# Toeplitz matrices of a token-mixing layer: 64 written rows per channel, or 16 table rows read at four offsets

## The chip, the cores and the metric

The kernel runs on one core of a Trainium2 chip. A core has TensorE (matmul), VectorE (DVE), ScalarE (ACT), GpSimd (POOL) and SyncE (SP), a fast memory SBUF of 128 partitions, accumulation banks PSUM, and 16 DMA engines that move data between DRAM and SBUF. SP computes nothing; it issues DMAs in the order of its program, and POOL issues some as well. The metric is the time of one execution in device microseconds.

## The reference

Four layers follow each other on an image batch x of shape (8, 56, 56, 192), all in float32. Before each layer x is group-normalized, and each layer's result is added to x. Layers 0 and 1 are gated Toeplitz layers and are the ones concerned here; layer 2 is a depthwise 7x7 convolution with an MLP, layer 3 is windowed attention.

A Toeplitz layer widens 192 channels to 576:

```python
p = silu(x @ p_w.T + p_b)
qv = silu(x @ q_w.T + q_b) * silu(x @ v_w.T + v_b)
a1 = _rpe_mlp(rpe_input, ...) * decay      # one value per lag and channel
a2 = _rpe_mlp(rpe_input, ...) * decay
o1 = _toeplitz(qv along w, a1)
o2 = _toeplitz(qv along h, a2)
out = (p * (o1 + o2)) @ o_w.T + o_b
```

For one channel c and one line of 56 points, `_toeplitz` gives `o[i] = sum_j a[i - j, c] * qv[j]`, with lags from -55 to 55. So each channel has its own 56x56 matrix in each of two directions, and every matrix is made from 111 values.

## The kernel before, in words

Samples are handled in pairs, four pairs in all; `j0` is 0 or 2 and names the two pairs that a stage works on. Layers are called L0 and L1 in the code.

**The stages of a Toeplitz layer.** `tno_qv` (here Q) loads x, normalizes it on ACT, multiplies by the weights `wq` on TensorE (L262, or L283 for the first tokens), adds the bias on DVE (L271, L290), takes SiLU on ACT (L300), multiplies q by v on POOL (L303) and stores the product to `qv` in DRAM through SP (L306). A store is issued just ahead of the ACT step of the unit after it. The tile for the product comes from a pool of three buffers.

`tno_toeplitz` (TZ) works through n = 0 to 17: nine blocks of 64 channels, and for each block d = 0 (along w) and d = 1 (along h). For each n it loads the products `q` (at even n with two DMAs, L378, in runs of 512 bytes; at odd n with one, L381) and the matrices `tm` (L388). For every channel TensorE takes two 56x32 pieces of its matrix as weights (L401): partition r holds row r of the Toeplitz matrix, so the piece `tm[rows, at:at + 32]` has a different shift in each partition. Two channels stand one below the other, in partitions 0 to 55 and 64 to 119. ACT copies the result (L408), DVE transposes it (L419, L421), POOL adds the second direction (L423) and stores the sum (L433). `tms` holds two tiles; the load for n + 2 is issued as n ends, after q's load for n + 2.

`tno_out` (O) loads the sums (L498) and x (L119), makes the gate p, multiplies, projects back with `ow`, adds x and stores.

**The tables.** `decay_tables` runs the small MLP for all 111 lags on TensorE and DVE, and writes `a`, a tile of 128 channels and 112 columns, from a pool of two buffers (`name="a"`, L186). There are five such tiles for each of two directions and two layers, 20 in all, the fifth of each with 64 channels. Each is stored to `tables[d]` in DRAM with one DMA (L198).

`expand_tables` then builds the matrices in DRAM with DMAs from DRAM to DRAM (L206): for 32 channels at once, 64 rows of 32 x 56 values, where row r is the table from lag entry r on. There are 18 such DMAs per table and four tables, 72 in all. Their source reads each run of 56 values (224 bytes) at its own offset.

**The order of the work.** `weave` interleaves generators by their estimated times: a lane of Q and O stages is run, and steps of TZ (or of `expand_tables`) are given out in proportion. In `tno_layers` the lanes are: Q(0,0) with the input statistics, the tables and `expand_tables`; then Q(0,2) with TZ(0,0); O(0,0) and Q(1,0) with TZ(0,2); O(0,2) and Q(1,2) with TZ(1,0); O(1,0) with TZ(1,2); and O(1,2) with the start of the convolution. In the first lane the order on each engine is set by a planner that goes by its own cost estimates. From the first TZ to the last, the four compute engines keep the order in which the code is written; SP's is still the planner's. Nothing reorders a queue at run time: an instruction that waits holds up all behind it on its engine.

Of the kernel before, what the change touches and what calls it, by code (L numbers as in the profile page):

```python
# [12 lines left out]
F32 = mybir.dt.float32  # L13
# [13 lines left out]
B, H, W, C = 8, 56, 56, 192  # L27
# [4 lines left out]
D1 = 576  # L32
# [11 lines left out]
class Net:  # L44
# [86 lines left out]

    def decay_tables(self, L, p, tables):

        nc, inp = self.nc, self.inp
        tv = p.tile([32, 111], F32, name="tv", bufs=1)
        nc.sync.dma_start(tv, inp["tvec"])
        pows = []
        for c in range(5):  # L140
            m = min(128, D1 - 128 * c)
            sl = p.tile([128, 1], F32, name="sl")
            nc.sync.dma_start(sl[:m], inp[f"{L}_slope"][128 * c : 128 * c + m, :])
            nc.vector.tensor_scalar(sl[:m], sl[:m], 0.0, 1.0, ALU.max, ALU.min)
            nc.vector.tensor_scalar(sl[:m], sl[:m], 1.0 - 0.95, 0.95, ALU.mult, ALU.add)
            pw = p.tile([128, 64], F32, name="pw", bufs=5)
            nc.gpsimd.memset(pw[:m, 0:1], 1.0)
            n = 1
            while n < 64:
                nc.vector.tensor_scalar(  # L150
                    pw[:m, n : 2 * n], pw[:m, 0:n], sl[:m], None, ALU.mult
                )
                n *= 2
                if n < 64:
                    sq = p.tile([128, 1], F32, name="sl")
                    nc.vector.tensor_mul(sq[:m], sl[:m], sl[:m])
                    sl = sq
            pows.append(pw)
        for d in range(2):
            t = f"{L}_t{d + 1}"  # L160
            w0 = p.tile([32, 2], F32, name="w0")
            nc.sync.dma_start(w0[:, 0:1], inp[f"{t}_w0"])
            nc.sync.dma_start(w0[:, 1:2], inp[f"{t}_b0"])
            ws = p.tile([32, 3, 32], F32, name="ws")
            nc.sync.dma_start(ws, inp[f"{t}_ws"])
# [5 lines left out]
            nc.sync.dma_start(bo, inp[f"{t}_bo"])  # L171
            h = p.tile([32, 111], F32, name="h")
            nc.vector.tensor_scalar(h, tv, w0[:, 0:1], w0[:, 1:2], ALU.mult, ALU.add)
            nc.vector.tensor_scalar(h, h, 0.0, None, ALU.max)
            for i in range(3):
                hp = self.bank2()[:32, 0, :111]
                nc.tensor.matmul(hp, ws[:, i, :], h, start=True, stop=True)
                h = p.tile([32, 111], F32, name="h")
                nc.vector.tensor_scalar(h, hp, bs[:, i : i + 1], 0.0, ALU.add, ALU.max)
            for c in range(5):  # L180
                m = min(128, D1 - 128 * c)
                ap = self.bank2()[:, 0, :111]
                nc.tensor.matmul(
                    ap[:m], wo[:, 128 * c : 128 * c + m], h, start=True, stop=True
                )
                a = p.tile([128, 112], F32, name="a")  # L186
                nc.gpsimd.memset(a[:m, 111:112], 0.0)
                back = view(pows[c][:m], 55, [[-1, 55]])
                for lo, hi, dec in ((0, 55, back), (55, 111, pows[c][:m, 0:56])):
                    nc.vector.scalar_tensor_tensor(  # L190
                        view(a[:m], 110 - lo, [[-1, hi - lo]]),
                        ap[:m, lo:hi],
                        bo[:m, c : c + 1],
                        dec,
                        ALU.add,
                        ALU.mult,
                    )
                nc.sync.dma_start(tables[d][128 * c : 128 * c + m, :], a[:m])  # L198

    def expand_tables(self, tables, mats):  # L200


        for tab, mat in zip(tables, mats):
            for n in range(D1 // 32):
# [159 lines left out]
    def tno_toeplitz(self, j0, mats, qv, o):  # L364
# [19 lines left out]
        def matrices(n):  # L384

            blk, d = divmod(n, 2)
            of = mats[d][2 * blk : 2 * blk + 2].rearrange("n p e -> (n p) e")
            nc.sync.dma_start(self.tms[n % 2][:, : 32 * H], of)  # L388

        def along(n, q, ot, g):  # L390


            d, tm = n % 2, self.tms[n % 2]
            pt = self.bank2()
            for hf in range(2):
                for j in range(4):
                    c = 4 * g + j
                    at = c * H + (28 if d else 24) * hf
                    for r in range(2):
                        rows = slice(64 * r, 64 * r + 56)  # L400
                        nc.tensor.matmul(  # L401
                            pt[32 * j : 32 * j + 32, r, hf * 224 : (hf + 1) * 224],
                            tm[rows, at : at + 32],
                            q[rows, :, 4 * c : 4 * c + 4],
                            start=True,
                            stop=True,
                        )
# [257 lines left out]
    def tno_layers(self, x0, x1, x2, gn, last):  # L665
# [3 lines left out]
        LS = ("L0", "L1")  # L669
        tables = [  # L670

            [self.dram.tile([D1 + 1, 112], F32, name=f"{L}_tab{d}") for d in range(2)]
            for L in LS
        ]
        mats = [
            [self.dram.tile([D1 // 32, 64, 32 * H], F32, name=f"{L}_mat{d}") for d in range(2)]
            for L in LS
        ]
        qvs = {
# [5 lines left out]
        with ExitStack() as ctx, ExitStack() as wqp:  # L685
# [4 lines left out]
            TZ = lambda i, j0: self.tno_toeplitz(j0, mats[i], qvs[j0], o[i])  # L690
            QT, OT, TZT = 25 * 2.25 * 5.3, 28 * 10.7, 8 + 72 * 3.2

            with tc.tile_pool(name="tab", bufs=2) as tab:
                stats = [self.input_stats(x0, gn[0], j, tab) for j in range(4)]
                for more in stats[0]:
                    pass
                first = Q(0, 0, tab)
                next(first)

                for n in range(14):  # L700
                    next(first)
                    next(stats[1], None)
                for more in stats[1]:
                    pass
                for n in range(10):
                    next(first)
                self.decay_tables("L0", tab, tables[0])
                for st in stats[2:]:
                    for more in st:
                        next(first)  # L710
                none = tab.tile([112, 512], F32, name="none", bufs=1)
                nc.gpsimd.memset(none, 0.0)
                for qv in qvs.values():
                    to = qv[:, T:].rearrange("n (p k) e -> p n (k e)", p=112)
                    nc.gpsimd.dma_start(to, view(none, 0, [[0, D1 // 32], [1, 512]]))
                self.decay_tables("L1", tab, tables[1])
                for t in tables:
                    for d in range(2):
                        nc.gpsimd.dma_start(t[d][D1:], none[:1, :112])
                lanes = [[(first, QT - 104.0)], [(Q(0, 2), QT)], [(O(0, 0), OT), (Q(1, 0), QT)]]  # L720
                lanes += [[(O(0, 2), OT), (Q(1, 2), QT)], [(O(1, 0), OT)], [(O(1, 2, False), OT)]]
                mat = (m for i in range(2) for m in self.expand_tables(tables[i], mats[i]))
                self.weave(lanes[0], mat, lanes[1][0][0], 72.0, 0.0, 0.88)
            in_order = tc.manual_schedule(engines=ENGINES)
            with tc.tile_pool(name="tz", bufs=1) as self.tz, in_order:
                self.tms = []
                for i in range(2):
                    tm = self.tz.tile([128, 32 * H + 8], F32, name=f"tm{i}")
                    nc.gpsimd.memset(tm, 0.0)
                    self.tms.append(tm)  # L730
                for n, tz in enumerate((TZ(0, 0), TZ(0, 2), TZ(1, 0), TZ(1, 2))):
                    self.weave(lanes[n + 1], tz, lanes[n + 2][0][0], TZT)
                    if n == 2:
# [910 lines left out]
```

## Time and profile before

Three runs took 5887.95, 5899.55 and 5893.0 us, a median of 5893.0 us. The profile below is of one further execution.

| | |
|---|---|
| median of three runs | 5893.0 us |
| the profiled execution's own time | 5873.81 us |
| its span in the trace | 5872.0 us |
| busy: TensorE, DVE, ACT, POOL | 91%, 40%, 39%, 38% |
| mean granted TensorE clock | 0.955 |
| bytes moved by DMA | 1119.25 MB, mean 191 GB/s |
| packets, and of these under 512 B | 1,139,528 and 342,528 |
| L206 (expansion) | 72 DMAs of 448 KB, issued from 149.1 to 462.2 us |
| L198 (table stores) | 20 DMAs, issued from 131.7 to 242.9 us |
| L388 (tm loads) | 72 DMAs of 896 KB, issued from 496.6 to 3187.0 us |
| L401 (Toeplitz matmuls) | from 512.4 to 3230.1 us |

The profile's times are microseconds from the start of the span. An instruction is named by engine, line, operation and tiles, out<-in; `SPq` is SP's queue, where the time of a DMA's line is that of issuing it, not of moving the data. What stands in brackets behind a group is the idle time of its engine before it and what ended it. "DMA share" is the mean busy share of the 16 DMA engines, counted by packets in flight, so that it can exceed 1. TensorE counts two instructions for each float32 matmul of the code.

### The profile page before, as it was taken

To read this page: it belongs to the slowest core of one execution; us is meant where nothing else is said; L and a number is where in the kernel's file an instruction comes from. 1 tells how busy PE (TensorE), PEld (TensorE's weight loads), DVE (VectorE), ACT (ScalarE), POOL (GpSimd) and SP (SyncE) were. 2 spreads that over 40 slices of the span, in tenths; PEclk is the share of its full clock that TensorE was granted. 3 is DMA by queue.
4 is the path that set the end of the run, shared out by engine and by line. 5 is a ranking of instruction groups with operands and counts; after the bars stand their busy time and mean duration, and the time that the engine had idled before them with its cause. 6 is when DMAs were issued, how large, how long until landed. Compare 5 with 4: busy or idle time off the path is not lost.

```text
span 5872.0 us, 143924 instructions
## 1 busy us (share of the span) xinstructions
PE 5361.4 (91%) x64672; PEld 3891.5 (66%) x64672; DVE 2362.3 (40%) x3770; ACT 2267.0 (39%) x2990; POOL 2209.1 (38%) x1529
## 2 busy tenths in 40 slices
PE   5998888899999999999888799989999999889897
PEld 2776666677777777777666678856665445666665
DVE  6434454233454233553344322331222322555565
ACT  2334454344454444554444322242323333333332
POOL 1334566466456565565666300000001001333332
PEclk8999998999999999999999899999999999999998
DMA  7799997788786788886999566634444223344442
GB/s 267 162 220 264 268 280 238 222 257 273 209 234 213 238 251 230 242 256 191 310 287 303 171 210 207 231 123 155 149 161 120 65 62 62 73 96 84 92 88 59
DMA packets 1139528, 1119.25 MB, mean 191 GB/s; under 512 B 342528, under 2 KB 1076736, under 8 KB 1123488
## 3 DMA queue, kind: packets, MB, share of 16 engines
q1 hardware_dynamic: 1103328, 909.05, 56.8%
q0 software_dynamic: 35584, 200.98, 8.9%
q8 instruction: 508, 8.32, 0.6%
q14 instruction: 108, 0.88, 0.1%
HBM read 753.79 MB, written 389.15 MB: 195 GB/s over the span
## 4 chain that ended last, share of the span: by engine, by line
PE 54%; DMA 11%; POOL 10%; issue 8%; DVE 8%; SPq 6%; ACT 3%; POOLq 0%; DVEq 0%; ACTq 0%
PE bank L262 12%; PE bank L953 6%; POOL s L423 4%; PE bank L814 4%; PE bank L1033 4%; PE bank L401 4%; DMA qv<-t 4%; PE bank L526 4%; PE bank L571 3%; DMA t<-L_sum 3%; PE bank L1047 3%; SPq L378 2%; POOL t L552 2%; SPq L388 2%; POOL t L303 2%
## 5 line engine op out<-in xcount | busy, mean ns | idle before, releaser
L262 PE MATMUL bank<-wq,t 128*128 128x256 f32 (+4 forms) x7680 | 1308.2, 379 | 101.4 <-DVE t L271 50.8
L262 PEld LDWEIGHTS bank<-wq,t 128*128 128x128 f32 (+2 forms) x7680 | 1021.3, 193 | 391.4 <-issue 113.3
L271 DVE TENSOR_TENSOR t<-bank,wq 128x1024 f32<-128x1024 f32 (+3 forms) x480 | 517.3, 1112 | 821.3 <-PE bank L262 559.1
L303 POOL TENSOR_TENSOR t<-t 128x1024 f32<-128x1024 f32 (+2 forms) x288 | 518.9, 1815 | 728.5 <-DMA qv<-t 395.4
L408 ACT COPY ot<-bank 128x896 f32<-128x896 f32 x576 | 492.7, 914 | 643.2 <-PE bank L401 377.1
L423 POOL TENSOR_TENSOR s<-s,ot 128x1568 f32<-128x1568 f32 x144 | 617.9, 4296 | 78.4 <-DVE ot L421 77.7
L401 PE MATMUL bank<-q,tm 56*32 56x224 f32 x18432 | 515.3, 359 | 72.4 <-DMA tm<-L_mat 23.1
L300 ACT ACTIVATE t<-t 128x2048 f32<-128x2048 f32 (+2 forms) x288 | 422.7, 1488 | 407.3 <-DVE t L271 393.1
L401 PEld LDWEIGHTS bank<-q,tm 56*32 56x32 f32 x18432 | 348.8, 107 | 203.8 <-issue 121.0
L552 POOL TENSOR_TENSOR t<-t,t 128x896 f32<-128x896 f32 x168 | 347.2, 2084 | 344.3 <-DMA t<-L_sum 164.3
L526 PE MATMUL bank<-t,wo 128*128 128x224 f32 x1792 | 394.8, 375 | 51.3 <-ACT t L505 22.7
L584 DVE SCALAR_TENSOR_TENSOR t<-bank,wo,t 128x448 f32<-128x448 f32 x112 | 76.4, 682 | 885.7 <-ACT t L580 417.3
L953 PE MATMUL bank<-z,w 128*128 128x448 f32 (+1 forms) x1344 | 417.5, 558 | 3.4 <-ACT h L962 3.4
L526 PEld LDWEIGHTS bank<-t,wo 128*128 128x128 f32 x1792 | 348.2, 201 | 88.5 <-issue 28.6
L545 ACT ACTIVATE t<-bank,wo 128x448 f32<-128x448 f32 x448 | 248.0, 635 | 396.9 <-PE bank L535 368.4
L571 PE MATMUL bank<-t,wo 128*128 128x224 f32 x1792 | 376.2, 364 | 0.0
L127 POOL DMA_DIRECT2D x<-x x64 | 36.7, 573 | 870.1 <-DVE x L984 840.0
L571 PEld LDWEIGHTS bank<-t,wo 128*128 128x128 f32 x1792 | 335.8, 193 | 33.0 <-issue 31.7
L814 PEld LDWEIGHTS bank<-xt,cm 113*112 113x112 f32 x3072 | 314.8, 180 | 45.6 <-issue 38.3
L419 DVE STREAM_TRANSPOSE s<-ot 128x1792 f32<-128x1792 f32 x144 | 292.3, 2034 | 112.2 <-DMA L_sum<-s 65.0
L814 PE MATMUL bank<-xt,cm 113*112 113x108 f32 (+2 forms) x3072 | 326.0, 266 | 8.3 <-ACT h L962 5.1
L953 PEld LDWEIGHTS bank<-z,w 128*128 128x128 f32 (+1 forms) x1344 | 183.7, 190 | 209.6 <-issue 200.2
(149 smaller groups left out, 6984.4 us busy)
## 6 DMA issues: line engine op xcount, KB each, us to landing
q<-qv SPq DMA_DIRECT2D x36, 3584.0 KB
q<-qv SPq DMA_DIRECT2D x72, 1568.0 KB
L_sum<-s POOLq DMA_DIRECT2D x288, 392.0 KB, 7.4
t<-L_sum SPq DMA_DIRECT2D x112, 1008.0 KB
qv<-t SPq DMA_DIRECT2D x192, 512.0 KB
cm<-in_L_cm SPq DMA_DIRECT2D x96, 896.0 KB
tm<-L_mat SPq DMA_DIRECT2D x72, 896.0 KB
x<-t POOLq DMA_DIRECT2D x112, 336.0 KB, 7.1
```

Of the source, the lines that this page charges most:

```text
L262: nc.tensor.matmul(pp[:m, b, 256 * j : 256 * j + k], x[rows, j, 2 if part else b, s : s + m], w[rows, part, c0 + c : c0 + c + k],  start=p ...
L271: nc.vector.tensor_add(z[:m, c : c + k, :], view(pp[:m], 0, [[1, k], [256, 4]]), view(bias[:m], c0 + c, [[1, k], [0, 4]]),)
L300: nc.scalar.activation(z[:m, :n, :], z[:m, :n, :], AF.Silu)
L303: nc.gpsimd.tensor_mul(prod[:m, :k], half[:, :, 0], half[:, :, 1])
L401: nc.tensor.matmul(pt[32 * j : 32 * j + 32, r, hf * 224 : (hf + 1) * 224], tm[rows, at : at + 32], q[rows, :, 4 * c : 4 * c + 4], start=Tr ...
L408: nc.scalar.copy(view(ot, 4 * (g % 4), [[16, 2], [32, 112], [1, 4]]), view(pt, 0, [[512, 2], [4, 112], [1, 4]]),)
L423: nc.gpsimd.tensor_add(to, to, view(of, 0, [[1, 28], [32, 56]]))
L526: mm(gs[c // 2][:, b, c % 2 * 256 : c % 2 * 256 + N], pw[:, 0, 128 * c : 128 * c + 128], xn[:, b], start=c % 2 == 0, stop=False,)
L552: gate.tensor_mul(to, to, pg)
L571: mm(P[:, b, :N], ow[:, c, 0:128], g[:, 4 * b + c], start=False, stop=c == 3 and b == 1)
L814: nc.tensor.matmul(pc[:, 128 * e + 4 * m0 : 128 * e + 4 * m1], cm[:113, e, k, :], xt[:, m0 - 1 + k : m1 - 1 + k, c + e, :], start=n == 0 a ...
L953: nc.tensor.matmul(phs[c][:, s, :TT], w0[rows, part, at : at + 128], z[rows, Z[2 if part else s], :], start=part == flip, stop=part != flip,)
```

## The change

`expand_tables`, its DRAM matrices and their 72 DMAs are gone. A table in DRAM now has, for each group of 32 channels, 16 rows (`TG`), and each row has 60 values per channel (`TW`): row g of a channel holds the table's entries from 4 g to 4 g + 59. `decay_tables` writes it straight from `a`, which has 120 columns now, with one DMA for each 32 channels: four for a tile of 128 channels, two for one of 64, 72 in all. The entries behind the 111 lags are zero.

Row r = 4 g + k of a Toeplitz matrix is row g of the table, read k values further on. So `matrices` loads `tm` with four DMAs, k = 0 to 3: each reads 32 table rows of 32 x 60 values, shifted by k values, into every fourth partition. A channel takes 60 columns of `tm` instead of 56, of which 56 are used; the tiles are no longer set to zero first.

```diff
+    TG, TW = 16, 60
...
-                a = p.tile([128, 112], F32, name="a")
-                nc.gpsimd.memset(a[:m, 111:112], 0.0)
+                a = p.tile([128, 4 * self.TG + 56], F32, name="a")
+                nc.gpsimd.memset(a[:m, 111:], 0.0)
...
-                nc.sync.dma_start(tables[d][128 * c : 128 * c + m, :], a[:m])
-
-    def expand_tables(self, tables, mats):
...
-                src = bass.AP(tab.tensor, tab.offset + n * 32 * 112, [[1, 64], [112, 32], [1, H]])
-                self.nc.sync.dma_start(mat[n].rearrange("p (c w) -> p c w", w=H), src)
-                yield 1.0
+                for n in range(m // 32):
+                    to = tables[d][self.TG * (4 * c + n) : self.TG * (4 * c + n + 1)]
+                    nc.sync.dma_start(
+                        to.rearrange("g (c w) -> c g w", w=self.TW),
+                        view(a[32 * n : 32 * n + 32], 0, [[4, self.TG], [1, self.TW]]),
+                    )
...
-            of = mats[d][2 * blk : 2 * blk + 2].rearrange("n p e -> (n p) e")
-            nc.sync.dma_start(self.tms[n % 2][:, : 32 * H], of)
+            row = 32 * self.TW
+            at = mats[d].offset + 2 * blk * self.TG * row
+            for k in range(4):
+                of = bass.AP(mats[d].tensor, at + k, [[row, 2 * self.TG], [1, row]])
+                nc.sync.dma_start(self.tms[n % 2][k:128:4], of)
...
-                    at = c * H + (28 if d else 24) * hf
+                    at = c * self.TW + (28 if d else 24) * hf
...
-                mat = (m for i in range(2) for m in self.expand_tables(tables[i], mats[i]))
-                self.weave(lanes[0], mat, lanes[1][0][0], 72.0, 0.0, 0.88)
+                self.weave(lanes[0], None, lanes[1][0][0])
...
-                    tm = self.tz.tile([128, 32 * H + 8], F32, name=f"tm{i}")
-                    nc.gpsimd.memset(tm, 0.0)
-                    self.tms.append(tm)
+                    self.tms.append(self.tz.tile([128, 32 * self.TW], F32, name=f"tm{i}"))
```

More of the change, by code (lines that the diff above doesn't have):

```diff
@@ L197, in decay_tables @@
                     )
-                nc.sync.dma_start(tables[d][128 * c : 128 * c + m, :], a[:m])
-    def expand_tables(self, tables, mats):
-        for tab, mat in zip(tables, mats):
-            for n in range(D1 // 32):
-                src = bass.AP(tab.tensor, tab.offset + n * 32 * 112, [[1, 64], [112, 32], [1, H]])
-                self.nc.sync.dma_start(mat[n].rearrange("p (c w) -> p c w", w=H), src)
-                yield 1.0
+                for n in range(m // 32):
[4 more added lines that the diff above has]
+                    )
     def input_stats(self, xs, gn, j, p):
@@ L670, in tno_layers @@
         tables = [
[L672 to L676, printed above, removed]
+            [
+                self.dram.tile([D1 // 32 * self.TG + 1, 32 * self.TW], F32, name=f"{L}_tab{d}")
+                for d in range(2)
+            ]
             for L in LS
@@ L689, in tno_layers @@
             O = lambda i, j0, woven=True: self.tno_out(LS[i], j0, x[i], gn[i], o[i], x[i + 1], gn[i + 1], woven)
-            TZ = lambda i, j0: self.tno_toeplitz(j0, mats[i], qvs[j0], o[i])
+            TZ = lambda i, j0: self.tno_toeplitz(j0, tables[i], qvs[j0], o[i])
             QT, OT, TZT = 25 * 2.25 * 5.3, 28 * 10.7, 8 + 72 * 3.2
@@ L718, in tno_layers @@
                     for d in range(2):
[L719 removed]
+                        nc.gpsimd.dma_start(t[d][D1 // 32 * self.TG :, :512], none[:1])
                 lanes = [[(first, QT - 104.0)], [(Q(0, 2), QT)], [(O(0, 0), OT), (Q(1, 0), QT)]]
                 lanes += [[(O(0, 2), OT), (Q(1, 2), QT)], [(O(1, 0), OT)], [(O(1, 2, False), OT)]]
[L722 to L723 removed]
+                self.weave(lanes[0], None, lanes[1][0][0])
             in_order = tc.manual_schedule(engines=ENGINES)
```

## Prediction

> **What bounds the kernel now.** I read the page's first table, then the stretch in which the change removes work (143 to 496 us), then the SP queue, where all its DMAs are issued.
>
> Busy time of the engines, from the page:
>
> ```profile
> span 5872.0 us, 143924 instructions
> PE 5361.4 (91%) x64672; PEld 3891.5 (66%) x64672; DVE 2362.3 (40%) x3770; ACT 2267.0 (39%) x2990; POOL 2209.1 (38%) x1529
> ```
>
> TensorE bounds it as a whole; only a stretch where TensorE waits can be shortened by moving less data. Windows of 50 us (columns: stretch, length, busy us of PE, PEld, DVE, ACT, POOL with instruction counts, granted clock, DMA share, GB/s):
>
> ```profile
> 250.00:300.00 50.00, 50.00 (x310) 39.95 (x306) 21.29 (x20) 23.18 (x24) 21.62 (x13) 1.00 0.81 191
> 300.00:350.00 50.00, 50.00 (x314) 40.19 (x314) 19.76 (x19) 18.49 (x18) 19.09 (x11) 1.00 1.13 229
> 350.00:400.00 50.00, 46.58 (x264) 35.47 (x262) 15.62 (x15) 19.03 (x21) 13.29 (x8) 0.93 1.12 220
> 400.00:450.00 50.00, 42.60 (x230) 32.95 (x231) 16.08 (x15) 15.46 (x15) 17.26 (x10) 0.90 1.16 222
> ```
>
> The same work (the first q/v stage) runs at 310 TensorE instructions per 50 us until the DMA share passes 1.1, and at 230 to 264 afterwards. TensorE in order of time and what POOL waited for from 300 to 500 us:
>
> ```profile
> 236.06 130.84 PE L262 MATMUL bank<-wq,t 128*128 128x128 f32 x800 [2.67 <-DVE a L190]
> 369.45 29.68 PE L262 MATMUL bank<-wq,t 128*128 128x128 f32 x160 [2.55 <-DVE t L271]
> 404.06 29.46 PE L262 MATMUL bank<-wq,t 128*128 128x128 f32 x160 [4.93 <-DVE t L271]
> 436.86 14.92 PE L262 MATMUL bank<-wq,t 128*128 128x128 f32 x80 [3.34 <-DVE t L271]
> 452.53 13.04 PE L262 MATMUL bank<-wq,t 128*128 128x128 f32 x80 [0.75 <-DVE t L271]
> 468.64 3.02 PE L262 MATMUL bank<-wq,t 128*64 128x128 f32 x16 [3.07 <-DVE t L271]
> 475.08 25.69 PE L262 MATMUL bank<-wq,t 128*128 128x256 f32 x144 [3.43 <-ACT t L245]
> 512.45 1.00 PE L401 MATMUL bank<-q,tm 56*32 56x224 f32 x16 [11.67 <-DMA tm<-L_mat]
> ...
> POOL t L303 <- DMA qv<-t: 99.9, 18, 8.6
> ```
>
> POOL's product (L303) waits 99.9 us for its old buffer's store; behind it ACT and DVE get late, and TensorE waits for banks (L271). The stores are late because they share SP's queue with the expansion (L206). SP from 520 us and in the tables (start, us in the instruction, what):
>
> ```profile
> 533.64 7.21 SPq L378 DMA_DIRECT2D q<-qv  x2
> 540.90 10.55 SPq L388 DMA_DIRECT2D tm<-L_mat  x1
> ...
> 560.32 0.42 SPq L388 DMA_DIRECT2D tm<-L_mat  x1
> ...
> 59.12 0.42 SPq L165 DMA_DIRECT2D ws<-in_L_t_ws  x1
> ...
> SPq L171 <- DMA t<-in_x: 1.8, 1, 1.8
> ```
>
> A DMA costs SP 0.42 us plus a gap when nothing is ahead; the one before L165 started at 58.66, so 0.47 from start to start. A tm load behind two q loads holds SP for 10.55 us: the descriptors ahead must drain first. The last line shows eight semaphores taking turns: the bo load waits for the t load eight DMAs before it in the queue.
>
> **What the skill says.** "DMA: Bandwidth & Descriptors", section "Why small descriptors are slow": a fixed overhead per packet. The trace agrees: a 224-byte packet of L206 took 16 ns (median of the trace's packet records), one of 512 B 27 ns, so 14 against 19 B/ns. The same page, "How a descriptor splits into AXI transactions": a start off a 256-byte boundary costs one more transaction. My estimate from it for 7680 B shifted by 4 to 12 B is 241 beats instead of 240. No aligned twin of L206 is in the trace; its sources were already shifted by single lags and show no high time. "Rules for kernel authors" there: coalesce small transfers, two transfers to disjoint partition halves share the same engines. So four tm loads gain no bandwidth.
>
> **The change, part by part.** *Removed: 72 expansions.* Each moves 448 KB in 2048 packets of 224 B. From 300 to 462 us some 49 are issued: 22 MB of about 36 MB moved there. Without them the DMA is at about half load and stores return before POOL needs them, as at 250 to 300 us. The first stage's L262 from 236.06 us on is 800+160+160+80+80+16 = 1296 instructions; at 50/310 = 0.161 us they take 209 us and end at 445.1 instead of 468.64+3.02 = 471.66: **-26.6 us**. Next late was Q(0,2)'s input (3.43 us before 475.08), whose load sat in the same blocked queue: **-3.4**. After it the wait of 11.67 us for the first tm: q and tm are loaded after the last qv store, which moves with TensorE, so I leave it.
>
> *Table stores: 20 DMAs become 72.* Each 128-row `a` has 4 stores of 512 packets of 240 B, 32 per engine: 0.6 us at 18 ns (between the 16 and the 25 to 30 ns of the 448-byte ones). SP needs 4 x 0.47 = 1.9 us per tile. `a` has two buffers, and the old stores already held the chain: DVE a at 137.06, 139.69, 142.75 us came 2.6 to 3 us apart per two tiles. Now SP sets 3.8 us per two tiles. In L0's tables (131 to 149 us) SP also issues 14 small weight loads and has no pause: 26 more DMAs x 0.47 = 12.2 us. Behind them on SP wait the L1 slope loads, L306 and L239; DVE, in order, waits for L143's data and for `a`, and L271 stands behind. TensorE needs the banks of the seventh and eighth tile, so 18 of 26: about +7.5 on the path. L1's (224 to 243 us) have slower old stores (3.9 us per pair, expansion packets ahead): +2.5. **+10**, bounds 0 (if other matmuls are put in between) to +24 (all of both, 2 x 12.2). The 9-column memset is nothing (0.1 us on POOL, beside DVE).
>
> *tm loads: 72 become 288.* Bytes: 960 for 896 KB, 65.5 kB more each. At 277 GB/s (2700 to 3000 us) that is 0.24 us. TZ(0,0) and TZ(1,2) run at a DMA share of 0.94 to 1.01, so 36 x 0.24 = 8.5 us there; in the two between (share near 0.8) it hides. Issue: 3 x 0.47 = 1.4 us of SP per load, 101 us in all. At even n the first of the four waits out the 10 us for q's descriptors; the other three go out while the engines still drain q's tail and the first quarter, so the stores behind (L306, L498) lose only the bytes. At odd n SP waits several us for POOL anyway (L306 waits 755.7 us in total). If that cover goes, 1.4 each. Four of eight semaphore turns now go to one load: the DMA eight places behind L378 comes three sooner. Matching packets to DMAs in queue order, old landings would hold back some 27 of the 791 SP DMAs of this stretch, mostly by 0.1 to 3 us and often inside waits that stay. TensorE waits for four semaphores instead of one, at 51 ns each, ahead of the work. **+8**, bounds 0 and +101.
>
> *Nothing:* removed tm memsets (2 x 1.6 us on POOL at 245 to 252 us, beside a TensorE that doesn't wait for POOL then); weights at 240 c instead of 224 c bytes (LDWEIGHTS is 107 ns for all shapes now).
>
> Sum: -26.6 - 3.4 + 10 + 8 = **-12 us**. The profiled execution took 5873.81 us (span 5872.0), 19 below the median of 5893.0; the difference is carried to the median: 5881. What a measurement here can tell from no change is 0.2%, 11.8 us: 5881.2 to 5904.8 is "same", so the likeliest stands on the edge.
>
> **Rivals.** *A, likeliest, 0.48:* as summed, 5869 to 5893; half of it faster, slightly more than half.
> *B, the tables take it back, 0.13:* both chains pay in full: -30 + 24 + 8 = +2, 5895. For it: SP had no pause in L0's tables. Against: TensorE needs only eight of ten tiles.
> *C, the three extra tm issues lie on the path, 0.21, slower:* the chain goes through L388 in about 15 steps (the page puts SPq L388 at 2% of the span), and TensorE waited for tm five times, 23.1 us. -30 + 10 + 8 + n x 1.4 exceeds zero from n = 9 on, and +11.8 from n = 17. At n = 36, all of TZ(0,0) and TZ(1,2), it is +38: 5931. For it: head-of-line blocking before stores. Against: the descriptors ahead outlast the issues.
> *D, the wait for the first tm also goes, or the tables hide, 0.18:* -12 - 10 or -12 - 12: 5869 to 5857. For it: L378's place on SP is a planner's choice and its model loses 72 transfers. Against: q's 3.2 MB still come after the last store.
> *E,* the stage isn't held by DMA: 250 to 300 us at the same work excludes it.
>
> Faster: 0.27 of A and D's 0.18 = 0.45. Same: 0.21 of A, 0.09 of B, 0.04 of C = 0.34. Slower: 0.17 of C, 0.04 of B = 0.21. The range 5857 to 5914 takes in D, A, B and the lower part of C.
>
> **What would show it.** Right: at the 300 to 450 us windows some 310 instructions per 50 us, DMA share near 0.6, POOL's wait for qv stores near 0; the first L401 near 494 us; the tables' `a` 3.8 us apart per pair; TZ stages as long as before within 8 us. Wrong: L388's three later issues far above 0.42 us, more tm waits on TensorE than 23 us, or a first L401 later than 505 us.

## The result and the profile after

The changed kernel takes 5858.9 us, the median of four runs (5851.37 to 5863.41), beside 5890.5 us for the kernel before on the same chip: a ratio of 0.9946, 95% interval 0.993 to 0.9963. It is 32 us faster. The forecast was 5881, with a range of 5857 to 5914 that holds the result near its lower end. The profiled execution took 5859.99 us. Its page begins:

```profile
span 5858.2 us, 144266 instructions
PE 5356.5 (91%) x64672; PEld 3886.7 (66%) x64672; DVE 2365.6 (40%) x3770; ACT 2269.0 (39%) x2990; POOL 2206.4 (38%) x1527
```

Each engine is busy for the same time as before to within 0.2%; what went is mainly idle time. The windows of 50 us, in the same columns as before:

```profile
250.00:300.00 50.00, 34.95 (x172) 25.63 (x173) 14.45 (x41) 8.16 (x6) 6.06 (x11) 0.73 0.51 84
300.00:350.00 50.00, 50.00 (x312) 39.68 (x309) 21.96 (x22) 21.95 (x24) 22.31 (x13) 1.00 0.68 196
350.00:400.00 50.00, 50.00 (x314) 39.97 (x313) 20.62 (x20) 22.78 (x24) 21.56 (x12) 1.00 0.45 136
400.00:450.00 50.00, 50.00 (x312) 40.20 (x313) 20.22 (x19) 22.41 (x24) 21.21 (x12) 1.00 0.37 110
...
POOL t L301 <- DMA qv<-t: 18.8, 5, 12.3
```

Two things are to be seen. From 300 us on, TensorE runs at full pace where it fell to 230 before, and POOL's wait for the old product's store (last line, the waits from 300 to 500 us) is 18.8 us instead of 99.9. But the window from 250 to 300 us, which was full before, is now the poor one: 172 instructions instead of 310. TensorE in order of time shows why:

```profile
152.59 0.60 PE L185 MATMUL bank<-h,wo 32*64 32x111 f32 x2 [2.68 <-DVE a L192]
154.51 4.58 PE L260 MATMUL bank<-wq,t 128*128 128x256 f32 x16 [1.33 <-issue]
...
243.17 2.69 PE L78 MATMUL bank<-gn_dev,pmat 128*128 128x2 f32 x12 [7.61 <-DVE gn_dev L92]
...
269.04 3.20 PE L260 MATMUL bank<-wq,t 128*128 128x128 f32 x16 [1.15 <-DVE a L192]
...
288.47 219.25 PE L260 MATMUL bank<-wq,t 128*128 128x128 f32 x1360 [0.46 <-DVE t L269]
```

The tables now delay TensorE twice, in L0 (to 154.51; 143.30 before) and in L1 (to about 276, against 236.06 before). DVE, which writes the tiles of the tables, waits there for stores of older tiles, and its tiles come 3.1 to 3.7 us apart:

```profile
148.58 0.45 DVE L192 SCALAR_TENSOR_TENSOR a<-bank,bo,pw 64x55 f32<-64x55 f32 x2 [3.27 <-DMA L_tab<-a]
151.98 0.46 DVE L192 SCALAR_TENSOR_TENSOR a<-bank,bo,pw 128x55 f32<-128x55 f32 x2 [2.95 <-DMA L_tab<-a]
```

From 288.47 us on TensorE runs without a pause to 507.7 us, into the first Toeplitz matmul: the waits of 3.43 us for Q(0,2)'s input and of 11.67 us for the first tm are both gone. But after the first two Toeplitz matmuls a new wait follows, for q:

```profile
513.19 3.24 PE L402 MATMUL bank<-q,tm 56*32 56x224 f32 x62 [4.98 <-DMA q<-qv]
```

In the kernel before, the first 64 ran in one piece from 512.45 to 515.69 us; here they end at 516.43. So the time of the first Toeplitz matmul flatters the changed kernel by some 5 us, which are found again in TZ(0,0).

The SP queue has the reasons, for the delay of the tables and for the early tm:

```profile
132.37 54.36 SPq L202 DMA_DIRECT2D L_tab<-a  x36
...
250.16 53.00 SPq L202 DMA_DIRECT2D L_tab<-a  x36
...
314.42 0.49 SPq L389 DMA_DIRECT2D tm<-L_tab  x1
...
335.88 2.40 SPq L389 DMA_DIRECT2D tm<-L_tab  x3
...
543.38 12.57 SPq L389 DMA_DIRECT2D tm<-L_tab  x4
...
558.87 2.75 SPq L389 DMA_DIRECT2D tm<-L_tab  x4
```

The planner placed all 36 table stores of a layer in one piece, which SP works through for 54 and 53 us, with the qv stores behind it. And it placed the first tm loads at 314 us; before they went out at 496.6.

The stages, measured from the first Toeplitz matmul of each (us; "tail" is all that follows the last Toeplitz matmul). e1 is the kernel before again, and e10 is it with a block of tiny matmuls ahead (below); e5 is the changed kernel again:

| trace | first Toeplitz matmul at | TZ(0,0) | TZ(0,2) | TZ(1,0) | TZ(1,2) | tail | span |
|---|---|---|---|---|---|---|---|
| before | 512.4 | 590.8 | 835.9 | 811.1 | 480.4 | 2641.4 | 5872.0 |
| e1_before | 515.3 | 592.9 | 833.5 | 811.8 | 483.4 | 2654.4 | 5891.4 |
| e10_pad256 | 519.0 | 593.1 | 836.9 | 809.6 | 485.4 | 2646.6 | 5890.6 |
| after | 507.7 | 594.2 | 827.5 | 804.6 | 488.9 | 2635.3 | 5858.2 |
| e5_after | 504.8 | 594.4 | 830.4 | 801.9 | 491.2 | 2635.8 | 5858.6 |
| e2_bufs | 470.2 | 594.1 | 828.8 | 805.7 | 487.8 | 2635.6 | 5822.2 |
| e3_onedma | 505.4 | 602.3 | 836.0 | 815.0 | 483.9 | 2651.1 | 5893.7 |
| e4_traffic | 576.0 | 595.3 | 824.0 | 802.0 | 492.6 | 2644.6 | 5934.4 |
| e7_one_inorder | 490.1 | 614.0 | 848.4 | 830.6 | 481.8 | 2646.2 | 5911.2 |
| e8_four_inorder | 488.7 | 615.8 | 850.4 | 829.1 | 484.7 | 2632.0 | 5900.7 |
| e9_pad104 | 516.8 | 589.0 | 836.0 | 810.0 | 486.5 | 2640.7 | 5878.9 |
| e11_onedma_pad104 | 505.8 | 600.7 | 833.9 | 815.3 | 490.3 | 2644.0 | 5890.1 |
| e12_after_pad152 | 503.2 | 594.0 | 830.8 | 805.4 | 488.2 | 2656.4 | 5877.9 |
| e13_bufs_pad64 | 468.8 | 592.1 | 829.9 | 802.4 | 496.0 | 2642.3 | 5831.5 |

Against the mean of the first three rows, the mean of "after" and e5 gains 9 us up to the first Toeplitz matmul, loses 2 us in TZ(0,0) (with the 5 us of the wait for q in it), gains 14 in the two stages that follow, loses 7 in TZ(1,2), and gains 12 in the tail, of which the change touches nothing. A single trace is only good to several us (the first three rows differ by 13 us in the tail), so the medians of many runs decide where they can.

### The profile page after: what moved, and what is told of

It is laid out like the page before. It is cut to its first block, busy times and chain, and to the rows that moved or that the text cites. A ratio compares the mean times of both kernels' runs of the same rounds, so it can differ in the third digit from the quotient of the medians.

```text
span 5858.2 us, 144266 instructions
## 1 busy us (share of the span) xinstructions
PE 5356.5 (91%) x64672; PEld 3886.7 (66%) x64672; DVE 2365.6 (40%) x3770; ACT 2269.0 (39%) x2990; POOL 2206.4 (38%) x1527
## 3 DMA queue, kind: packets, MB, share of 16 engines
q8 instruction: 509, 8.34, 0.6%
## 4 chain that ended last, share of the span: by engine, by line
PE 57%; POOL 6%; SPq 6%; DMA 5%; DVE 5%; issue 3%; ACT 2%; POOLq 0%; DVEq 0%; ACTq 0%
PE bank L260 9%; PE bank L950 6%; PE bank L811 5%; PE bank L527 4%; PE bank L1030 4%; PE bank L572 4%; PE bank L402 4%; SPq L389 3%; PE bank L1044 3%; POOL s L424 2%; PE bank L1224 2%; PE bank L536 2%; PE bank L575 2%; SPq L376 2%; PE bank L1171 2%
## 5 line engine op out<-in xcount | busy, mean ns | idle before, releaser
L260 PE MATMUL bank<-wq,t 128*128 128x256 f32 (+4 forms) x7680 | 1286.6, 375 | 66.8 <-DVE t L269 36.3
L260 PEld LDWEIGHTS bank<-wq,t 128*128 128x128 f32 (+2 forms) x7680 | 1006.5, 191 | 348.1 <-issue 110.5
L402 PE MATMUL bank<-q,tm 56*32 56x224 f32 x18432 | 525.6, 365 | 81.6 <-DMA tm<-L_tab 26.8
```

Of the source, the lines that this page charges most:

```text
L260: nc.tensor.matmul(pp[:m, b, 256 * j : 256 * j + k], x[rows, j, 2 if part else b, s : s + m], w[rows, part, c0 + c : c0 + c + k],  start=p ...
L402: nc.tensor.matmul(pt[32 * j : 32 * j + 32, r, hf * 224 : (hf + 1) * 224], tm[rows, at : at + 32], q[rows, :, 4 * c : 4 * c + 4], start=Tr ...
```

## The experiments

**Both kernels again.** e1 is the kernel before, with nothing changed.

> The kernel before once more, unchanged, for a second profile of it. The shown profile of before took 5873.81 us, 17 us less than the median of its runs, and its difference to the profile after is 13.7 us where the medians differ by 31.6. Theory (that profile was a quick execution, and the gain is real): ratio 1.000 within 0.002, and a new profile whose span is near 5890 us; the first Toeplitz matmul again near 512 us, so that the excess lies after it. Rival (profiles run quicker than timed runs, for both kernels): the new profile is near 5874 us again, with the last Toeplitz matmul near 3230 us.

Measured: 5886.2 us beside 5888.8, ratio 0.9994 (0.9981 to 1.0007). The first profiled execution of the kernel before (5873.81 us) was a quick one of its kind; e1's took 5893.86. e5 is the changed kernel.

> The kernel after once more, unchanged, for a second profile. Between the profiles of before and after the stages differ by -5 us up to the first Toeplitz matmul, by -8 and -7 us in TZ(0,2) and TZ(1,0), by +8 us in TZ(1,2), and by -6 us after the last Toeplitz matmul. Theory (all of these but the last are properties of the program): the same marks within 2 us each, first matmul near 507, the stages 594, 828, 805 and 489 us long; the stretch after them, whose order of work is the same in both kernels, differs by up to 13 us as it did between the two profiles of before. Rival (they are scatter between executions): the stages differ from the first profile by as much as they do from before.

Measured: 5850.1 us beside 5881.6, ratio 0.995 (0.9936 to 0.9963). The result stands, and its stages come out within 3 us of those of the first trace (2 were expected).

**The tables' buffers.** e2 gives the table tile ten buffers instead of two, so that no tile waits for stores to land; the 72 stores stay.

```diff
-                a = p.tile([128, 4 * self.TG + 56], F32, name="a")
+                a = p.tile([128, 4 * self.TG + 56], F32, name="a", bufs=10)
```

> The kernel after with ten buffers for the table tile a in place of two: no tile waits for the stores of the tile two before it. Theory (the tables take long since each tile waits until its four stores have landed, and DVE, TensorE and everything behind them on SP wait with it): TensorE's wait of 24.6 us at the table matmuls goes, the first Toeplitz matmul comes at 475 to 485 us in place of 507.6, and the time falls from 5858.9 to about 5825 to 5835 us, ratio 0.989 to 0.991. Rival (SP's issuing of 72 stores at 0.5 us each, ahead of the qv stores and the small loads, is what delays): at most 8 us gained, 5851 to 5859 us, with the qv stores still behind 36 stores in one piece.

Measured: 5819.6 us, ratio 0.9891 (0.9876 to 0.9907): 1.1% below the kernel before, and in the profiled spans 36 us below the changed kernel (5822.2 and 5858.2). It beats both. Its first Toeplitz matmul comes 37 us earlier than the changed kernel's, and a wait of 4.93 us for q follows it there too. First the waits of the changed kernel from 128 to 310 us, then TensorE in e2:

```profile
POOL a L189 <- DMA L_tab<-a: 49.8, 12, 9.7
...
PE bank L185 <- DVE a L192: 24.6, 9, 5.6
```

```profile
138.67 33.23 PE L260 MATMUL bank<-wq,t 128*128 128x256 f32 x192
...
177.51 34.58 PE L260 MATMUL bank<-wq,t 128*128 128x256 f32 x192 [0.35 <-ACT gn_std L95]
...
235.34 234.95 PE L260 MATMUL bank<-wq,t 128*128 128x128 f32 x1440
```

The first Q now continues at 138.67 and 235.34 us, as early as or earlier than in the kernel before (143.30 and 236.06), and 1440 matmuls follow without a pause. SP still issues 36 stores in one piece there, now in 31.90 us:

```profile
131.53 31.90 SPq L202 DMA_DIRECT2D L_tab<-a  x36
```

So most of the loss was the tile waiting for its stores to land, which also stretched SP's piece to 54 us. The order on TensorE, ACT and SP is the same in both traces up to the first Toeplitz matmul; on DVE and POOL the tiles of the tables come earlier. The rival keeps a part: between the two tables e2 still takes 85.2 us (138.67 to 223.83), where the kernel before took 77.6 (143.30 to 220.85). TensorE waits 7.69 us there for the statistics (7.61 in the changed kernel, 0.98 before), while DVE waits, up to 4.07 us at a time, for slopes whose loads stand behind the 36 stores on SP. The tables make up for it: TensorE is through L0's 4.6 us earlier than in the kernel before, and L1's take it 3.7 us less. In e2 the 36 stores of L0 land from 137.8 to 168.5 us, 0.88 us apart. The packets of 240 bytes have a median of 18 ns, as the forecast assumed, but a mean of 31 ns in this stretch. 120 KB in 0.88 us is 140 GB/s, against 219 to 287 GB/s in the slices of the changed kernel's page from 440 to 1320 us. Four stores at 0.88 us are 3.5 us per tile, the pace at which the tiles follow each other in the changed kernel. The Trainium skill, "DMA: Bandwidth & Descriptors", section "Anatomy of one DMA — SWDGE (gpsimd) path", puts about 2 us of fixed cost to a DMA and most of it into confirming that the last byte has landed. These stores go out from SP, but agree as far as they can: in the changed kernel the quickest of L0's 36 landed 2.4 us after its issue began, the slowest 7.1, the median 4.3. Two buffers with four stores each can't hide that.

**The traffic put back.** e4 is the changed kernel with 72 DMAs of the old expansion's shape, from the tables into an array that nobody reads, woven in as before. It does more work than either kernel.

```diff
-                self.weave(lanes[0], None, lanes[1][0][0])
+                mat = (m for i in range(2) for m in self.expand_traffic(tables[i], spare[i]))
+                self.weave(lanes[0], mat, lanes[1][0][0], 72.0, 0.0, 0.88)
```

> The kernel after with the 72 expansions put back as mere traffic: the same number and shape of copies from table to a spare array that nothing reads, given out as before. Theory (the first stage was slowed by this traffic, and the first tm loads came late behind it): from 310 instructions per 50 us TensorE falls to 230 to 270 in the second half of the stage, about 27 us lost, the wait of about 12 us for the first tm is back, and the time rises by 35 to 45 us to 5894 to 5904 us, ratio 1.001 to 1.002. Rival (only the dependence of tm on matrices in DRAM cost time, not the traffic): the stage keeps its pace, and at most 12 us are lost, 5871 us or less, ratio 0.997 or less.

Measured: 5936.1 us, ratio 1.0086 (1.0073 to 1.01), 77 us above the changed kernel; the signs are those expected, the price is about twice the expected one. A window and a wait of TensorE in its timeline:

```profile
350.00:400.00 50.00, 39.83 (x224) 30.68 (x222) 13.58 (x14) 17.79 (x21) 14.73 (x9) 0.91 1.18 224
```

```profile
576.00 3.24 PE L412 MATMUL bank<-q,tm 56*32 56x224 f32 x64 [10.21 <-DMA tm<-L_tab]
```

All the old signs come back with the traffic: a DMA share of 1.18, 224 instructions in 50 us, POOL's wait for the qv stores (158.9 us from 300 to 560 us), and the wait for the first tm, which is again loaded late. So the expansions caused both. Whether they did so by their bytes or by their place in SP's queue, e4 doesn't separate. That the price is 68 us up to the first Toeplitz matmul, and not the 44 that the step and the tm wait had been worth (26.6 + 17.6, below), goes with their place: the tables' stores hold them back, so that only three of the 72 are issued before 297 us and the last at 525, where before they ran from 149.1 to 462.2 us. This was not tested by itself.

**One load or four.** e3 is the changed kernel with one DMA per tm load instead of four, of the same bytes.

```diff
-            for k in range(4):
-                of = bass.AP(mats[d].tensor, at + k, [[row, 2 * self.TG], [1, row]])
-                nc.sync.dma_start(self.tms[n % 2][k:128:4], of)
+            of = bass.AP(mats[d].tensor, at, [[row, 2 * self.TG], [1, 4], [1, row]])
+            nc.sync.dma_start(self.tms[n % 2], of)
```

> The kernel after with one DMA per tm load: the same rows, shifts and 960 KB, but one instruction and one semaphore in place of four. Theory (the three further issues are hidden behind descriptors that are still being drained): 0 to 4 us gained, 5855 to 5859 us, ratio about 0.994. Rival (three issues of 0.5 us or more per load lie on SP's path in the Toeplitz stages, and hold back the stores behind): 25 us or more gained, 5834 us or less, most of it in the stages of TZ(0,0) and TZ(1,2).

Measured: 5889.5 us, ratio 1.0006 (0.9996 to 1.0016): fewer DMAs, and 30 us slower than the changed kernel. Neither expectation came true; both had the one load at least as fast. TZ(0,2), TZ(1,0) and TZ(1,2) have the lengths of the kernel before to within 5 us, and so has the tail; TZ(0,0) is 10 us longer than there. POOL's waits in TZ(0,2), e3 first, then the changed kernel:

```profile
POOL t L552 <- DMA t<-L_sum: 84.2, 9, 17.5
POOL t L301 <- DMA qv<-t: 82.7, 10, 16.0
```

```profile
POOL t L301 <- DMA qv<-t: 69.1, 8, 16.4
POOL t L553 <- DMA t<-L_sum: 64.5, 8, 15.2
```

In these two lines POOL waits 33 us less in the changed kernel. The order on SP differs between the two kernels (a second trace of the same kernel repeats it DMA for DMA): with one load the planner put the next input loads right behind tm, as in the kernel before; with four it put them behind qv stores or sum loads, and in TZ(1,2) it moved q and tm ahead of a sum load. To take the order out, e7 and e8 hold SP to the order of the code in these stages (with ten table buffers), and differ only in one load against four.

```diff
 ENGINES = (
...
+    mybir.EngineType.SP,
```

> The kernel after with ten buffers for a, SP kept in the order in which the code is written during the Toeplitz stages, and one DMA per tm load. It is the partner of e8_four_inorder: both issue the same DMAs in the same order but for this load. Theory (what sped up TZ(0,2) and TZ(1,0) in the kernel after is the planner's other order on SP, in which input loads stand behind the qv stores or the sum loads, and not the four loads as such): this one is as quick as its partner in TZ(0,0), TZ(0,2) and TZ(1,0), within 3 us each. Rival (four separate loads with their own semaphores let TensorE or SP go on sooner): this one is slower by 6 to 10 us in each of these stages, as e3_onedma was against the kernel after.

> The kernel after with ten buffers for a and SP kept in the order in which the code is written during the Toeplitz stages, with the four tm loads. Theory (issue of the three further loads is hidden, 0 to 8 us in all four stages): within 8 us of e7_one_inorder, slower if anything. Rival (1.4 us per load on SP's path): 25 us or more slower than e7_one_inorder. Against e2_bufs, which has the same tables and the planner's order on SP, it shows what that order is worth: from -10 to +15 us.

Measured: 5913.0 us with one load, ratio 1.0062 (1.0048 to 1.0075), and 5902.7 with four, 1.0037 (1.0025 to 1.0049). In the four stages four loads are 1.8, 2.0, -1.5 and 2.9 us longer, 5 us together, from one trace of each; the same sum differs by 7 us among the first three rows of the table. As a whole four loads are 10 us faster, with a tail that is 14 us shorter (more on it below). So under one order the cost of four loads is about 5 us, too little to be told from none, and the shorter TZ(0,2) and TZ(1,0) of the changed kernel don't come from the loads themselves; the planner's other order is what remains of the difference between it and e3. The order of the code is poor for SP, in both:

```profile
PE bank L402 <- DMA tm<-L_tab: 79.7, 8, 20.6
```

```profile
PE bank L403 <- DMA tm<-L_tab: 86.7, 10, 20.5
```

TensorE waits 80 and 87 us for tm (e7, e8; changed kernel 26.8), and e8 is 83 us slower than e2, from which only SP's order divides it; -10 to +15 had been expected of that order.

**The tail.** After the last Toeplitz matmul DVE, ACT, POOL and SP have the same order in all these kernels, and the work is untouched. Still the kernels with four loads had 2632 to 2636 us there and those with one load 2641 to 2654 (e4, four loads, 2644.6). What they share beside the loads is the number of TensorE's instructions: the four semaphore waits per load add 105 up to the end of the last Toeplitz stage (66,593 before, 66,698 after, 66,589 in e3). TensorE's instructions are themselves brought by DMA; the page of the changed kernel has a queue for them:

```profile
q8 instruction: 509, 8.34, 0.6%
```

8.34 MB in 509 packets is 16.4 KB each, and at 64 bytes for an instruction (the Trainium skill, "Perfetto Trace Analysis", section "The 4-stage abstract model") 256 instructions; TensorE's records number 130,356, which is 509.2 times 256. So theory P: how TensorE's code falls into these blocks decides how the last stages run. The test puts tiny matmuls ahead of everything, where TensorE is idle; each adds four instructions, and the order of every engine is otherwise unchanged.

```diff
         tc, nc = self.tc, self.nc
+        b = self.bank2()
+        for i in range(26):
+            nc.tensor.matmul(b[:, 0, 0:2], self.pmat[:, 0, :], self.pmat[:, 0, 0:2], start=True, stop=True)
         LS = ("L0", "L1")
```

e9 is the kernel before with 26 of them (104 instructions), e10 the same with 64 (256, a whole block), e11 is e3 with 26.

> The kernel before with 26 tiny matmuls (104 TensorE instructions by the trace's way of counting, four to a matmul) ahead of everything, where TensorE is idle; the order of every engine is otherwise unchanged. Theory P (the position of TensorE's instructions in the program sets how the last stages run; the changed kernel has 105 more by the end of the last Toeplitz stage): the tail after the last Toeplitz matmul falls from 2641-2654 to 2632-2637 us, the whole time by 8 to 18 us, ratio 0.997 to 0.9985. Rival N (position is nothing; the tail differs for a reason of DMA or of chance): tail 2641 to 2654 us, ratio 0.9995 to 1.0005.

> The kernel before with 64 such matmuls, 256 TensorE instructions, ahead of everything. Theory P with a period of 256 instructions (16 KB, as the packets of the instruction queue): position as before, tail 2641 to 2654 us, ratio 0.9995 to 1.0005. Rival N: the same. If e9 is shorter and this one too, it isn't the position modulo 256 that matters.

> The changed kernel with one DMA per Toeplitz load (e3) and the same 26 matmuls ahead of everything. Theory P: tail 2632 to 2637 us instead of e3's 2651, time 5872 to 5880, ratio 0.997 to 0.9985. Rival N: tail 2641 to 2654, ratio 0.9996 to 1.0016 as e3.

Measured: e9 5876.0 us, ratio 0.9979 (0.9971 to 0.9987); e10 5891.7 us, 1.0004 (0.9995 to 1.0013); e11 5879.4 us, 0.998 (0.9972 to 0.9989), against 1.0006 for e3. More work made the kernel before faster by 0.2%, and a whole block changed nothing, as theory P has it. The tails of the single traces (2640.7 and 2644.0) didn't fall as far as expected; the times over 20 and 22 runs are the firmer evidence. The mirror is e12: the changed kernel with 38 tiny matmuls (152 instructions), which with its own 105 makes 257, so the position of the kernel before. And e13 puts e2 into a third position with 16 of them (64 instructions).

> The changed kernel with 38 tiny matmuls (152 TensorE instructions) ahead of everything: by the end of the last Toeplitz stage it then has 105 + 152 = 257 instructions more than the kernel before, so the same position within 256. Theory P: it loses what the changed kernel got from its position, 10 to 14 us: 5861 to 5871 us beside a kernel before of 5889, ratio 0.9965 +- 0.001 instead of 0.995. Rival N' (only e9 and e11 happened to gain, or the gain comes from having matmuls at the start): ratio 0.994 to 0.9955, as the changed kernel.

> The changed kernel with ten table buffers (e2) and 16 tiny matmuls (64 TensorE instructions) ahead: a third position within 256 for the fastest kernel so far. Theory P only says that it may move by up to 0.2% either way: 5808 to 5832 us, ratio 0.987 to 0.991; no change beyond 0.05% says that the two positions are alike. Rival N': 0.9891.

Measured: e12 5870.0 us, ratio 0.9977 (0.997 to 0.9984); e13 5833.3 us, 0.9914 (0.99 to 0.9928), 14 us above e2, though the two intervals just overlap. e12 keeps all that the change does and loses some 0.3%, 16 to 18 us (0.9977 against 0.995 and 0.9946). Its stages stay as they were up to 3221.5 us (3222.9 in the changed kernel), and its tail is 21 us longer (this execution, of 5880.35 us, was 10 us above the median of its kind). So by this pair about half of the change's 32 us came from the position of TensorE's instructions, and 13.5 us (0.23%, interval 0.16% to 0.30%) from what it does. e9 and e11 say more of these 13.5 us. They are the kernel before and the changed kernel with one load, at positions within five instructions of each other, and their ratios are the same (0.9979 and 0.998). So with one load, where SP keeps the order of the kernel before in the Toeplitz stages, the change brings nothing. What it brings with four loads thus goes with SP's other order, and the removed expansions are paid back by the tables and by a longer TZ(0,0).

What the position acts on can be read in the timeline of the attention stage. The changed kernel, a group of 64 matmuls (L1254), and one of 32 of another line ahead of it and behind it:

```profile
4964.60 1.54 PE L1224 MATMUL bank<-xa,Wq 128*32 128x224 f32 x32
...
4967.38 0.92 PE L1254 MATMUL bank<-f,f 32*64 32x49 f32 x48
4971.25 0.68 PE L1254 MATMUL bank<-f,f 32*64 32x49 f32 x16 [2.95 <-issue]
4971.86 2.84 PE L1224 MATMUL bank<-xa,Wq 128*32 128x224 f32 x32
```

The group of L1254 breaks off after 48, and TensorE stands for 2.95 us with nothing that the profile shows to wait for. I numbered all of TensorE's records, weight loads and semaphore waits included, in order of start, and took the number modulo 256 of each instruction that follows such a wait of TensorE ("issue") in the last 900 us:

| trace | waits put down to issue | us | of these at 193 or 194 modulo 256 |
|---|---|---|---|
| before | 43 | 42.4 | 42 |
| e9_pad104 | 61 | 59.0 | 61 |
| after | 55 | 52.6 | 55 |
| e12_after_pad152 | 42 | 47.2 | 42 |
| e2_bufs | 51 | 46.0 | 51 |

They lie at one point of each block, the same in every kernel, whatever stands ahead. The reading is that TensorE waits there for its next block of instructions. The packets of the instruction queue agree: of these 252 waits 249 ended 1.2 to 2.0 us after a packet had landed, and only 18% of all matmuls of these stretches start in that interval after one. This stage goes through 256 instructions in 5.2 us (173 blocks in the last 900 us; 240 in the 2700 us from 500 us on).

The sum of these waits doesn't sort the kernels: the faster e9 has more of it than before, and the second trace of the kernel before has 52.9 us to the first one's 42.4. The granted clock is a better lead. The traces record it as full or half, in stretches of 3.4 us and multiples of it. A half stretch of 6.83 us begins at 4970.44 us, in the last us of the wait above, and in it the 32 matmuls of L1224 take 2.84 us instead of 1.54 (last and first line). Over the 14 traces the length of the tail goes with the time at half clock in it, from 205 us in e9 to 247 us in e12: the correlation is 0.82, with 0.51 us of tail for each us at half clock. The timed runs agree. The 48 of the kernel before beside e9 are about 4 us shorter for each 0.001 of mean granted clock, and that mean is 0.9547 in e9 and 0.9541 in e11 (0.9524 and 0.9516 without their shift), 0.9519 in e10, and 0.9541 in e12 (0.9557 without). So the position may act through the waits that bring on half clock. This is not shown: no run holds the clock fixed, and the clock may be low because TensorE waits more, not the other way round. Which places are the bad ones stays open.

## Why the forecast was right where it was, and where it was wrong

The range held, and that owes much to luck: the sum of -12 us comes near to what the change itself does only because errors cancel, and the position of TensorE's instructions, which the forecast didn't have, brought about as much again. The likeliest value was 22 us too high. By its own steps:

- **Removed expansions, -26.6: right in size and mechanism.** The pace from 300 us on is 312 to 314 instructions per 50 us, as the step assumed (310), and 1360 matmuls in 219.25 us are 0.161 us each. e4 shows the cause by bringing it back.
- **Q(0,2)'s input, -3.4: right.** That wait is gone.
- **The wait for the first tm, left in place: wrong.** The 1296 matmuls end at 484.5 us (288.47 + 1216 x 0.1612), and the first Toeplitz matmul comes 23 us later, where it was 40.8 us in the kernel before (471.66 to 512.45): -17.6 with the 3.4 above and 2.5 of pace, of which the new wait of 4.98 us for q takes 5 back in TZ(0,0). The step took q and tm as bound to the last qv store; for q that was right, for tm not. The planner, with no expansions on SP, had put the first eight tm DMAs at 314 to 341 us. Rival D had this gain at 10 us; net of the wait for q it is 6.7 (11.67 less 4.98).
- **Table stores, +10 with bounds 0 to 24: wrong, the largest error.** The 1296 matmuls that began at 236.06 us now begin at what would be 275.6 us at full pace (288.47 less 80 x 0.161): +39.5. It has three parts: 11.2 in L0's tables (143.30 to 154.51), 14.6 in L1's (15.2 us before, from 220.85 to 236.06; 29.8 now, from 245.79), and 13.7 between them, where the qv stores, an x load and the slope loads stand behind the 36 stores. I priced SP's issue (1.9 us per tile), and took 0.6 us per store in the DMA engines; they took 0.88, four to a tile, and it is the landing of these that a pool of two buffers waits for. So two tiles took about 7 us where the forecast, which saw the two buffers but let SP set the pace, had 3.8, and its bound fell with the mechanism. (Within the step, 18 x 0.47 is 8.5, not 7.5.) e2 removes the wait and gets 37 us back, with the 72 stores still there. The first Toeplitz matmul at 507.7 us instead of 494 was the sign that I had named for an error here.
- **tm loads, +8 with bounds 0 and 101: of the right order for the loads alone, wrong for what they did to the order on SP.** The three extra DMAs cost some 5 us in all four stages, no more than the scatter (e7, e8). In the changed kernel the four stages together are 5 us shorter than in the traces of the kernel before, which is within that scatter too; what both of its traces repeat is that TZ(0,2) and TZ(1,0) are shorter and TZ(1,2) longer, by 5 to 9 us each. SP's order, which changed with the loads, is what is left to explain it. The 8 us that I had named as a sign of being right were about that. TensorE's waits for tm, with more than 23 us named as a sign of being wrong, were 26.8 us. (The DMA share that I gave for TZ(0,0), 0.94 or more, is 0.91 over the whole stage.)
- **Not in the sum at all: the tail, -12 in the traces and 12 to 18 by the pairs of medians.** The instructions that four waits per load add to TensorE moved the code of the stages behind, and e12, which moves it back, loses about as much. Nothing in the views of the kernel before that I read hinted at it; its waits put down to issue at one point modulo 256 were in the trace.

The sum of -12 is close to the 13.5 us that remain with the position taken out (e12), by these errors: +29 in the tables against -14 at the first tm and -13 in the stages (-5 instead of +8, with the wait for q in it). Rival B (the tables take the gain back) had the right place and too low a price (24 for what became 39.5). Rival C, the one for slower, is refuted by the stages: n x 1.4 us should have shown in them. At 543.38 us the four loads hold SP for 12.57 us, where before one took 10.55; at 558.87 us four took 2.75, where one took 0.42. The result lies in the interval of rival D (whose own two sums are 5871 and 5869, and 5859 for both together), of which one mechanism was right and the other, that the tables would hide, was the opposite of what happened.

## What to carry to other kernels

A store that is cut into more and smaller pieces is priced by when its buffer comes free, that is by the landing of the last piece, and not by what its issue costs; count the buffers as well as the instructions. Where a planner orders a queue, a change to the number of DMAs can move work that it doesn't touch, so compare the order of the queue and not only its content, and separate the two with a variant that holds the order fixed. When a stage that was not touched changes by 0.2%, shift the instructions of the bounding engine by part of a block before you believe in any other cause; here that alone made a difference of this size. Compare the mean granted clocks of the runs as well.

## What the runs showed of the hardware that was not expected

- TensorE's instructions come in blocks of 16.4 KB, and in a stage that goes through 256 of them in 5.2 us TensorE waits, for up to 3 us in the changed kernel, at the same point of a block (all but one of 252 such waits in five traces), and 249 of these waits end 1.2 to 2.0 us after a packet of the instruction queue has landed. Shifting the code by 104 instructions was worth -0.2% of the whole kernel, by 256 nothing, and by 152 from the better position +0.3%.
- Stores of 512 packets of 240 bytes landed 0.88 us apart when SP issued them back to back, with a median of 18 ns but a mean of 31 ns per packet.
- The granted clock goes to half for stretches of 3.4 us and multiples of it, in which the same 32 matmuls took 2.84 instead of 1.54 us; over 14 traces the length of the last stages goes with the time at half clock in them (correlation 0.82).
- One load of 960 KB and four of 240 KB, each to every fourth partition, differ by about 5 us over 72 loads under one order on SP, no more than the same stages scatter (7 us).
